# Finding the places of routed results: scatters into four small tables in place of one-hot products

## The chip, the cores and the metric

The kernel runs on one core of a Trainium2 chip. The metric is the device time of one execution in microseconds (us). The profile is of one such execution, and its span is the time from the first to the last instruction that it records.

## What is computed

The input x has 16 sequences of 512 tokens with 256 features. The layer normalises x and adds to x an attention (16 heads of 16, each token sees itself and the 128 before it) and a mixture of experts:

```python
xn = _layernorm(x, axis=-1)
x = x + attn(xn, Wq, bq, Wk, bk, Wv, bv, Wo, bo) + ffn(xn, ...)
# ffn:
logits = xt @ gate_w.T
_, idx = jax.lax.top_k(logits + beta, K)            # K = 2 of E = 8 experts
probs = jax.nn.sigmoid(jnp.take_along_axis(logits, idx, axis=-1))
c = jnp.zeros((B, E), xt.dtype).at[jnp.arange(B)[:, None], idx].add(probs)
h = jax.nn.silu(g) * u                              # g, u: 256 -> 512 of each expert
eo = jnp.einsum('bem,emh->beh', h, down_proj_w)     # 512 -> 256
combined = jnp.einsum('beh,be->bh', eo, c)
return (combined + shared_out).reshape(B0, S0, H0)  # shared_out: one FFN for all tokens
```

There are 8192 tokens, so 16384 results (token, chosen expert) have to be computed, each to be weighted with its probability.

## The kernel before, in words

**Stages.** `norm` (lines 204 to 271) normalises the sequences in groups of three, writes the rows to `xn_d` in HBM, and makes values and routing logits. `route` (325 to 465) chooses the experts. `attention` (625 to 679) works through 64 groups (16 sequences, four head groups each) in five steps per group. `early` (833) computes the shared FFN of one sequence. `experts` (856 to 957) runs over NB = 135 blocks: the results are sorted by expert, every expert's run is rounded up to whole blocks of 128 slots, and a block gathers its 128 rows of `xn_d` by `source` (line 877), turns them on PE, multiplies with the expert's weights (897, 915), and scatters 128 rows of results into `y_d` by `target` (922). `y_d` has two rows for every token. `endings` (961 to 1000) reads for each sequence the sums so far (`acc`) and in two halves its rows of `y_d`, multiplies these rows by `prob` (968), adds both rows of each token (972), and stores.

**How places are found in `route`.** Lines 336 to 408 give for every token and choice a slot number (block times 128 plus lane); token number t x 128 + p and choice k stand in partition p, column (t, k) of `slots`. What the blocks need is the inverse: for each lane and block, which result it is. Lines 429 to 457 get it with 128 products: for each (t, k) VectorE (DVE) builds `hot_l` (128 x 128, 1 where the lane is the result's, line 444) and `hot_b` (128 x 135, the result's number where the block is the result's, line 448), and PE adds `hot_l` transposed times `hot_b` into one bank, `found` (434). Lines 459 to 465 make `target` and `source` of it; a slot that got no result has zero there and is sent to a row that nobody reads.

**The order of the work.** Everything is issued from one loop over `attention` (1054 to 1064), four turns a step, 1304 turns in all, and every engine takes its instructions in the built order. In each turn beside attention's own work: `background` (normalisation, then routing) is advanced one step in five of every eight turns, until it ends; `filling` is advanced `pace` = 0.918 steps; `endings` one step. `filling` (1008 to 1027) runs shared FFNs of whole sequences, 24 steps each, until routing has ended, then all the experts (810 steps), then the remaining shared FFNs; a shared FFN of the sequence that attention works on is held back until attention's part is stored. `endings` starts when the experts are through, eight turns a sequence. When the loop is over, the rest of `filling` and then of `endings` is issued (1067 to 1070). A scheduler that builds the program may move an instruction on its engine within what dependences allow.

**Queues that matter.** GpSimd (POOL) issues the indirect DMAs (877, 922), and between them copies each group's values into place (`spread_values`, 502), adds `bo` to a first `acc` (816), and does the endings' arithmetic. The value copies are needed by PE's products with the values (605), a whole group of 20 turns later. SyncE (SP) issues all other DMAs in order, a wait included. `y_in` has two buffers, `acc` four. A large part of route's scratch lies in the same buffers as the weights (`part_tile`).

Of the kernel before, what the change touches and what calls it, by code (L numbers as in the profile page):

```python
# [41 lines left out]
def block_kernel(ctx: ExitStack, tc: tile.TileContext, a: dict, out: bass.AP):  # L42
# [130 lines left out]
    lane = count("lane", [[1, P]], P)  # L173
    block_no = count("block_no", [[1, NB]], NB)

    result_no = count("result_no", [[1, 2], [2 * P, TT]], 2 * TT, by=2, base=1)
    result_no = result_no.rearrange("p (k t) -> p k t", k=2)
# [133 lines left out]
    prob = const.tile([P, 2, TT], FP, tag="prob", name="prob")  # L311
    expert = const.tile([P, NB], I32, tag="expert", name="expert")
    source = const.tile([P, NB], I32, tag="source", name="source")
    target = const.tile([P, NB], I32, tag="target", name="target")
    no_token = one.tile([P // 2, D], FP, tag="no_token", name="no_token")
    nc.gpsimd.memset(no_token, 0.0)
    nc.sync.dma_start(out=xn_d[TT * P :], in_=no_token)
# [7 lines left out]
    def route():  # L325
# [32 lines left out]
        nc.vector.reciprocal(prob, prob)  # L358

# [43 lines left out]
        for k in range(2):  # L403
# [5 lines left out]
        part = one.tile([P, 2, TT, 2], I32, tag="r_part", name="r_part")  # L409
        nc.vector.tensor_single_scalar(part[:, 0], slots, 7, op=ALU.logical_shift_right)  # L410
        nc.vector.tensor_single_scalar(part[:, 1], slots, P - 1, op=ALU.bitwise_and)
        where = small[:, 2:].rearrange("p a k t -> p a (k t)").rearrange(
            "p a (t k) -> p a t k", k=2
        )
        nc.vector.tensor_copy(where, part)

# [10 lines left out]
        yield  # L427

        found = bank_b()
        ready = []  # L430

        def add_ready():
            for t, k, hot_l, hot_b in ready:
                nc.tensor.matmul(
                    found[:, :NB], lhsT=hot_l, rhs=hot_b,
                    start=t == 0 and k == 0, stop=t == TT - 1 and k == 1,
                )
            ready.clear()

        for t in range(TT):  # L440
            pairs_of = []
            for k in range(2):
                hot_l = six.tile([P, P], FP, tag="hot_l", name="hot_l")
                nc.vector.tensor_scalar(  # L444
                    hot_l, lane, where[:, 1, t, k : k + 1], None, ALU.is_equal
                )
                hot_b = six.tile([P, NB], FP, tag="hot_b", name="hot_b")
                nc.vector.tensor_scalar(  # L448
                    hot_b, block_no, where[:, 0, t, k : k + 1], result_no[:, k, t : t + 1],
                    ALU.is_equal, ALU.mult,  # L450
                )
                pairs_of.append((t, k, hot_l, hot_b))
            add_ready()
            ready.extend(pairs_of)
            if t % 2:
                yield
        add_ready()
        unused = first
        nc.vector.tensor_scalar(
            unused, found[:, :NB], 0.0, unused_no, ALU.is_equal, ALU.mult  # L460
        )
        nc.vector.tensor_tensor(unused, unused, found[:, :NB], ALU.add)
        nc.vector.tensor_scalar_add(unused, unused, -1.0)
        nc.vector.tensor_copy(target, unused)
# [391 lines left out]
    def experts():  # L856
# [53 lines left out]
        def half_down(i, half):  # L910
# [8 lines left out]
            if half == 1:  # L919
                y = three.tile([P, D], FP, tag="y", name="y")  # L920
                nc.scalar.copy(y, sums.pop(i)[:, :D])  # L921
# [39 lines left out]
    def endings():  # L961
        added = []

        def add():
            b, half, acc, y = added.pop()
            tiles = slice(NT // 2 * half, NT // 2 * (half + 1))
            weight = prob[:, :, b * NT : (b + 1) * NT][:, :, tiles].rearrange("p k t -> p t k")
            nc.gpsimd.tensor_tensor(
                y, y, weight.unsqueeze(3).to_broadcast([P, NT // 2, 2, D]), ALU.mult
            )  # L970
# [164 lines left out]
```

## Time and profile before

| | us |
|---|---|
| median of three runs | 1988.27 (1985.82 to 1989.53) |
| the profiled execution | 1989.47 |
| its span | 1987.8 |
| one-hot stage, first `hot_l` to last `hot_b` | 436.7 to 538.6 |
| first expert matmul (897) | 548.5 |
| last scatter into `y_d` starts | 1778.6 |
| endings' arithmetic on POOL (968, 972) | 1784.7 to 1981.1 |
| attention's last reciprocal (622) | 1958.0 |

In a profile line, L448 is line 448 of the kernel; PE is the matrix engine and PEld its weight loads, ACT is ScalarE, SPq and POOLq are DMAs issued by these engines. A group's line gives the engine, the operation, the output and inputs with shapes, xcount, then busy time in us, mean duration in ns, and after the second bar the idle time ahead of it with what ended it. A float32 matmul shows as two records. Busy times of matmuls overlap a little, since they are pipelined. The chain that ended last lies to 88% of the span on PE.

### The profile page before, as it was taken

Reading aid. Unit: us, or ns where it says so; the run is one execution under the profiler, and the core shown is the slowest. Engines: PE = TensorE matmul, PEld = TensorE weight load, DVE = VectorE, ACT = ScalarE, POOL = GpSimd, SP = SyncE. Lnnn points to the kernel's source line nnn. Section 1 sums busy time; section 2 is a strip of 40 time slices with the busy share of each in tenths; the row PEclk is TensorE's granted clock in tenths of the full one; section 3 lists DMA queues with packets and bytes.
Section 4 is the critical chain, followed back from the end, with each engine's and each line's share of the span. In section 5 each row is a group of like instructions: output and inputs, shape, how many; then the busy total and the mean of one; then the engine's idle time right before and its main releaser. Section 6 shows DMA issues by size and latency. Waiting matters only on the chain.

```text
span 1987.8 us, 35311 instructions
## 1 busy us (share of the span) xinstructions
PE 1916.6 (96%) x12011; PEld 1654.5 (83%) x12011; DVE 1211.1 (61%) x3912; ACT 684.6 (34%) x1752; POOL 605.8 (30%) x765
## 2 busy tenths in 40 slices
PE   7899999999899999999999999999999999998985
PEld 4677767767789999999989899998989899985763
DVE  5767756599945565555555566555655565555652
ACT  3333323321133333333333333333333333332320
POOL 5212212210022222222222323222222222228884
PEclk9899999999999999999999999999999999999997
DMA  7634434341257676777676777777676777757774
GB/s 198 196 120 154 151 88 133 128 124 35 59 183 245 204 233 229 223 243 220 208 235 219 223 234 232 218 251 212 217 226 216 225 235 233 217 182 215 228 238 147
DMA packets 355773, 386.58 MB, mean 194 GB/s; under 512 B 118528, under 2 KB 262976, under 8 KB 355584
## 3 DMA queue, kind: packets, MB, share of 16 engines
q1 hardware_dynamic: 342624, 348.82, 55.9%
q0 software_dynamic: 12960, 35.41, 5.5%
q8 instruction: 98, 1.61, 0.3%
q14 instruction: 91, 0.75, 0.1%
HBM read 307.67 MB, written 68.09 MB: 189 GB/s over the span
## 4 chain that ended last, share of the span: by engine, by line
PE 88%; DVE 8%; POOL 1%; DMA 1%; issue 1%; ACT 0%; SPq 0%; POOLq 0%; DVEq 0%; ACTq 0%
PE a L897 24%; PE a L557 13%; PE b L915 12%; PE c L605 12%; PE a L764 9%; PE b L789 5%; PE b L777 3%; PE b L255 3%; PE a L524 2%; PE a L514 2%; PE b L887 2%; DVE hot_b L448 1%; DVE den L622 1%; DVE hot_l L444 1%; DVE probs L546 1%
## 5 line engine op out<-in xcount | busy, mean ns | idle before, releaser
L897 PE MATMUL a<-xgT,w 128*128 128x128 f32 x4320 | 548.7, 276 | 1.9 <-DVE maxima L546 1.0
L897 PEld LDWEIGHTS a<-xgT,w 128*128 128x128 f32 x4320 | 526.9, 193 | 12.7 <-issue 8.5
L550 ACT ACTIVATE probs<-probs,maxima 128x160 f32<-128x160 f32 (+4 forms) x1024 | 346.2, 401 | 528.8 <-DVE maxima L546 508.4
L546 DVE CUSTOM_DVE_ANT_0 probs<-a,window 128x160 f32<-128x160 f32 (+4 forms) x1024 | 254.1, 297 | 235.4 <-PE a L557 225.0
L605 PEld LDWEIGHTS c<-turned,spread_v 128*128 128x128 f32 x2048 | 308.9, 191 | 58.2 <-issue 42.6
L605 PE MATMUL c<-turned,spread_v 128*128 128x160 f32 (+4 forms) x2048 | 338.1, 290 | 10.5 <-DVE ctxT L623 10.1
L557 PE MATMUL a<-kT,spread 128*128 128x160 f32 (+4 forms) x2048 | 323.2, 295 | 0.0
L557 PEld LDWEIGHTS a<-kT,spread 128*128 128x128 f32 x2048 | 290.4, 192 | 33.2 <-issue 25.0
L877 POOL DMA_INDIRECT xg<-xn_d,source x135 | 132.9, 984 | 472.3 <-PE b L887 416.6
L915 PE MATMUL b<-w,hr 128*128 128x256 f32 x1080 | 271.7, 381 | 0.0
L622 DVE RECIPROCAL den<-den 64x512 f32<-64x512 f32 x64 | 214.1, 3346 | 85.3 <-ACT den L617 82.7
L764 PE MATMUL a<-xT,shared 128*128 128x512 f32 x480 | 242.0, 609 | 11.5 <-DMA xT<-xT_d 11.5
L596 DVE STREAM_TRANSPOSE turned<-probs 128x480 f32<-128x480 f32 (+1 forms) x256 | 161.8, 632 | 104.9 <-ACT probs L550 101.5
L502 POOL COPY spread_v<-v 32x256 f32<-32x256 f32 x256 | 101.4, 397 | 373.8 <-PE c L605 219.9
L922 POOL DMA_INDIRECT y_d<-y,target x135 | 132.4, 981 | 266.3 <-ACT y L921 236.5
L915 PEld LDWEIGHTS b<-w,hr 128*128 128x128 f32 x1080 | 189.8, 190 | 19.6 <-issue 2.6
L753 DVE SCALAR_TENSOR_TENSOR hr<-hr,a 128x512 f32<-128x512 f32 x135 | 91.8, 680 | 136.4 <-ACT hr L752 127.8
L789 PE MATMUL b<-shared,h 128*128 128x256 f32 x512 | 133.1, 392 | 4.4 <-DVE acc L794 2.8
L752 ACT ACTIVATE hr<-a 128x512 f32<-128x512 f32 x135 | 79.9, 592 | 149.5 <-PE a L897 142.2
L764 PEld LDWEIGHTS a<-xT,shared 128*128 128x128 f32 x480 | 83.8, 195 | 50.7 <-issue 36.1
L754 DVE SCALAR_TENSOR_TENSOR hr<-hr,a 128x512 f32<-128x512 f32 x135 | 91.8, 680 | 45.9 <-PE a L897 43.0
L789 PEld LDWEIGHTS b<-shared,h 128*128 128x128 f32 x512 | 94.4, 196 | 20.0 <-DVE acc L794 3.5
(141 smaller groups left out, 1701.1 us busy)
## 6 DMA issues: line engine op xcount, KB each, us to landing
w<-in_gp SPq DMA_DIRECT2D x135, 512.0 KB
w<-in_up SPq DMA_DIRECT2D x135, 512.0 KB
w<-in_dp SPq DMA_DIRECT2D x135, 512.0 KB
acc_d<-acc SPq DMA_DIRECT2D x32, 512.0 KB
acc<-acc_d SPq DMA_DIRECT2D x32, 512.0 KB
y_in<-y_d SPq DMA_DIRECT2D x32, 512.0 KB
xT<-xT_d SPq DMA_DIRECT2D x30, 512.0 KB
xn_d<-xn SPq DMA_DIRECT2D x16, 512.0 KB
```

Of the source, the lines that this page charges most:

```text
L546: nc.vector.tensor_tensor_reduce(out=to, in0=ps, in1=window[:, WIN - n :], scale=-SCALE, scalar=-MASKED, op0=ALU.add, op1=ALU.min, accum_o ...
L550: nc.scalar.activation(to, to, AF.Exp, bias=least, scale=-1.0)
L557: nc.tensor.matmul(ps, lhsT=spreads[group % 2][:, u].rearrange("p g q -> p (g q)"), rhs=w["kT"][:, group // 2, f:e], start=True, stop=True,)
L596: nc.vector.transpose(moved(pT, Q * blocks[0] + P * first, [[WIN, n], [P, SEEN], [1, Q]]), moved(pr, 0, [[WIN, n], [Q, SEEN], [1, Q]]),)
L605: nc.tensor.matmul(av[:, Q * k : Q * k + n], lhsT=spread_v[s][:, k], rhs=pT[:, WIN * k : WIN * k + n], start=k == ORDER[0], stop=k == ORDE ...
L622: nc.vector.reciprocal(den[mine], den[mine])
L764: nc.tensor.matmul(ps, lhsT=wt[:, c, ts(m, P)], rhs=xT[:, c], start=c == 0, stop=c == KC - 1,)
L789: nc.tensor.matmul(po[t][:, :D], lhsT=h[m][:, ts(t, P)], rhs=wd[:, m], start=m == 0, stop=m == MC - 1,)
L877: nc.gpsimd.indirect_dma_start(out=g, out_offset=None, in_=xn_d, in_offset=bass.IndirectOffsetOnAxis(ap=source[:, i : i + 1], axis=0),)
L897: nc.tensor.matmul(hidden[i][which][:, ts(m, P)], lhsT=weights[i, which][:, c, ts(m, P)], rhs=turned[i][:, c], start=c == 0, stop=c == KC - 1,
L915: nc.tensor.matmul(po[:, :D], lhsT=made[i][:, ts(m, P)], rhs=weights[i, 2][:, m], start=m == 0, stop=m == MC - 1,)
L922: nc.gpsimd.indirect_dma_start(out=y_d, out_offset=bass.IndirectOffsetOnAxis(ap=target[:, i : i + 1], axis=0), in_=y, in_offset=None,)
```

## The change

Routing no longer builds one-hot matrices. Each result's pair (number, weight) is written by an indirect DMA into its slot's row of a table in HBM. There are 128 such scatters of 128 rows with 8 bytes, issued by POOL two per background step; they go round four tables, so that a table is written by every fourth. The tables are filled with zeros at the start of the kernel. After the scatters SP reads the four tables back into two tiles, DVE adds them (every slot is written in one table, the others hold zero), PE transposes the sum in four pieces, and DVE makes `target`, `source` and a new `share_of` (the weight of each slot) from that. Route has 84 background steps for the 45 before. Since the weight is now known for each slot, ACT scales a block's rows as it takes them from the bank, and the multiply at the endings is dropped. The diff, cut to its core:

```diff
+    pairs = const.tile([P, TT, 2, 2], FP, tag="pairs", name="pairs")
+    nc.gpsimd.tensor_copy(pairs[:, :, :, 0], result_no.rearrange("p (t k) -> p t k", k=2))
...
+    NE = NB + NB % 2
+    share_of = const.tile([P, NE], FP, tag="share_of", name="share_of")
+    nothing = one.tile([NE // 2, 4 * P], FP, tag="nothing", name="nothing")
+    nc.gpsimd.memset(nothing, 0.0)
+    tables = [dram.tile([NE * P, 2], FP, tag=f"table{i}", name="table") for i in range(4)]
+    by_row = lambda t: t.rearrange("(j x) n -> j (x n)", j=NE // 2)
+    for t in tables:
+        nc.sync.dma_start(out=by_row(t), in_=nothing)
...
         nc.vector.reciprocal(prob, prob)
+        nc.vector.tensor_copy(pairs[:, :, :, 1], prob.rearrange("p k t -> p t k"))
...
-        part = one.tile([P, 2, TT, 2], I32, tag="r_part", name="r_part")
-        nc.vector.tensor_single_scalar(part[:, 0], slots, 7, op=ALU.logical_shift_right)
-        nc.vector.tensor_single_scalar(part[:, 1], slots, P - 1, op=ALU.bitwise_and)
-        nc.vector.tensor_copy(where, part)
...
-        for t in range(TT):
-            pairs_of = []
-            for k in range(2):
-                hot_l = six.tile([P, P], FP, tag="hot_l", name="hot_l")
-                nc.vector.tensor_scalar(
-                    hot_l, lane, where[:, 1, t, k : k + 1], None, ALU.is_equal
-                )
-                hot_b = six.tile([P, NB], FP, tag="hot_b", name="hot_b")
-                nc.vector.tensor_scalar(
-                    hot_b, block_no, where[:, 0, t, k : k + 1], result_no[:, k, t : t + 1],
-                    ALU.is_equal, ALU.mult,
-                )
-                pairs_of.append((t, k, hot_l, hot_b))
-            add_ready()
-            ready.extend(pairs_of)
-            if t % 2:
-                yield
+        for t in range(TT):
+            for k in range(2):
+                nc.gpsimd.indirect_dma_start(
+                    out=tables[(2 * t + k) % len(tables)],
+                    out_offset=bass.IndirectOffsetOnAxis(ap=slots[:, t, k : k + 1], axis=0),
+                    in_=pairs[:, t, k], in_offset=None,
+                )
+            yield
+        yield
+        rows = [part_tile(i, "rows")[: NE // 2] for i in range(2)]
+        for i, t in enumerate(tables):
+            nc.sync.dma_start(out=rows[i // 2][:, ts(i % 2, 4 * P)], in_=by_row(t))
+        for _ in range(4):
+            yield
+        low, high = (r[:, : 4 * P] for r in rows)
+        for r in rows:
+            nc.vector.tensor_tensor(r[:, : 4 * P], r[:, : 4 * P], r[:, 4 * P :], ALU.add)
+        entry = rows[0][:, 4 * P :]
+        nc.vector.tensor_tensor(
+            entry.rearrange("j (n h x) -> j h x n", n=2, h=2),
+            low.rearrange("j (h x n) -> j h x n", n=2, h=2),
+            high.rearrange("j (h x n) -> j h x n", n=2, h=2), ALU.add,
+        )
+        yield
+        found = bank_b()[:, : 2 * NE]
+        for i in range(4):
+            nc.tensor.transpose(
+                found[:, ts(i, NE // 2)], entry[:, ts(i, P)], ident[: NE // 2, : NE // 2]
+            )
+        yield
...
-                nc.scalar.copy(y, sums.pop(i)[:, :D])
+                nc.scalar.mul(y, sums.pop(i)[:, :D], share_of[:, i : i + 1])
...
-            weight = prob[:, :, b * NT : (b + 1) * NT][:, :, tiles].rearrange("p k t -> p t k")
-            nc.gpsimd.tensor_tensor(
-                y, y, weight.unsqueeze(3).to_broadcast([P, NT // 2, 2, D]), ALU.mult
-            )
             for k in range(2):
                 nc.gpsimd.tensor_tensor(acc[:, tiles], acc[:, tiles], y[:, :, k], ALU.add)
```

## The prediction

> **What bounds the kernel now.** I read the page first: its busy totals and the span in 40 slices (49.7 us each).
>
> ```profile
> PE 1916.6 (96%) x12011; PEld 1654.5 (83%) x12011; DVE 1211.1 (61%) x3912; ACT 684.6 (34%) x1752; POOL 605.8 (30%) x765
> ...
> DVE  5767756599945565555555566555655565555652
> POOL 5212212210022222222222323222222222228884
> ```
>
> PE is the bound nearly everywhere. Two places differ: slices 8 to 10, where DVE is full and POOL idle, and the last four, where POOL is at 8. The busy time by stretches, columns PE, PEld, DVE, ACT, POOL, then granted clock, DMA share and GB/s:
>
> ```profile
> 333.00:436.00 103.00, 102.92 (x481) 75.66 (x480) 78.39 (x222) 32.62 (x87) 22.01 (x33) 1.00 0.34 102
> 436.00:540.00 104.00, 95.66 (x541) 77.86 (x541) 101.64 (x400) 20.37 (x52) 3.88 (x10) 0.95 0.21 64
> 563.65:676.05 112.40, 112.00 (x810) 104.86 (x809) 61.29 (x202) 42.34 (x108) 28.62 (x37) 1.00 0.70 229
> ```
>
> The middle row is the stage that the change replaces: DVE 101.6 of 104 us. The groups by line say with what, and show the other lines the change touches:
>
> ```profile
> L502 POOL COPY spread_v<-v 32x256 f32<-32x256 f32 x256 | 101.4, 397 | 373.8 <-PE c L605 219.9 <-DMA y_d<-y,target 75.7 <-issue 39.1
> L972 POOL TENSOR_TENSOR acc<-acc,y_in 128x512 f32<-128x512 f32 x64 | 80.9, 1267 | 18.3 <-issue 11.5 <-DMA acc<-acc_d 2.8
> L968 POOL TENSOR_TENSOR y_in<-y_in,prob 128x1024 f32<-128x1024 f32 x32 | 60.8, 1901 | 27.7 <-DMA y_in<-y_d 27.4
> L448 DVE TENSOR_SCALAR hot_b<-block_no,r_f,result_no 128x135 f32<-128x135 f32 x128 | 43.8, 342 | 0.0
> L434 PE MATMUL b<-hot_b,hot_l 128*128 128x135 f32 x256 | 42.0, 286 | 0.8 <-DVE hot_b L448 0.8
> L444 DVE TENSOR_SCALAR hot_l<-lane,r_f 128x128 f32<-128x128 f32 x128 | 35.0, 273 | 0.0
> ```
>
> The timeline of POOL in two short windows prices an indirect DMA (columns: start, duration, line; in brackets the idle time before):
>
> ```profile
> 545.16 0.94 POOL L877 DMA_INDIRECT xg<-xn_d,source  x1 [0.31 <-issue]
> 546.41 0.95 POOL L877 DMA_INDIRECT xg<-xn_d,source  x1 [0.30 <-issue]
> ...
> 837.33 0.97 POOL L922 DMA_INDIRECT y_d<-y,target  x1 [1.15 <-ACT y L921]
> 838.35 0.39 POOL L502 COPY spread_v<-v 32x256 f32<-32x256 f32 x1
> 842.29 1.26 POOL L502 COPY spread_v<-v 32x256 f32<-32x256 f32 x3 [3.55 <-DMA y_d<-y,target]
> ```
>
> Two back to back are 1.25 us apart, and after a scatter the second value copy (L502) starts only when it has landed: 842.29 - 837.33 = 5.0 us. Last, the tail after the final matmul (1967.9):
>
> ```profile
> 1968.38 0.37 SPq L827 DMA_DIRECT2D acc_d<-acc  x1
> 1972.11 0.37 SPq L813 DMA_DIRECT2D acc<-acc_d  x1
> 1976.17 4.92 POOL L972 TENSOR_TENSOR acc<-acc,y_in 128x512 f32<-128x512 f32 x4 [8.15 <-issue]
> 1981.11 0.38 SPq L827 DMA_DIRECT2D out<-acc  x1
> ```
>
> One sequence's sums go out and back, then one store: 20 us. The execution took 1989.5 us, 1.7 over its span, and lies at the top of the three runs (median 1988.3). The sum below is made against this execution.
>
> **Part 1: the one-hot products go.** Removed: 78.8 us of DVE (43.8 + 35.0) and 42.0 us of PE records. In the stretch 436 to 540 PE executed 541 records, 256 of them these. The other 285 at the 0.214 us of the row above (102.92 / 481) are 61 us: 43 us gained. Adding up PE's columns in built order (eight records of 512 columns take 3.43 us, so 1.67 ns per column of a two-record matmul, times 1.04 for what PE loses in a loaded stage) gives the same picture: 161 us of columns lie between the first hot matmul (437.3) and the changed kernel's first expert matmul, so unhindered that falls at 437 + 168 = 605. It comes later than now (548.5) only because three more shared FFNs are put before it (part 3).
>
> **Part 2: 128 scatters on POOL's queue.** Each is one DMA_INDIRECT. A scatter into a table waits for the one before into the same table, so at most four are under way: the pitch is the larger of 1.27 us (0.97 + 0.30) and a quarter of the landing, 5.0/4 = 1.25. I take 1.3. The trace has no 8-byte scatter; the bounds are 0.97 (no gap) and 9.0/4 = 2.25 (the longest landing in the trace, 1040.10 to 1049.09), and I stay by the commonest row. 128 x 1.3 = 166 us on an engine that PE's schedule gives about 140 (102 turns of the main loop at 1.4).
>
> What is queued behind them is the point: POOL runs in order, and the value copies L502 that every head group's PE products (L605) need stand between the scatters. In the built order the copies for groups 12, 13, 14, 15 and 16 come after 4, 38, 82, 120 and 128 scatters, and each waits until the scatters before it have landed (3.7 us beyond its own first copy, with the copies 5 us). Scatters start when the slots are ready (cast L408, 434.2). Copies ready: group 12 at 445; group 13, 34 x 1.3 + one bias add L816 (2.4) + 5 later, 497; group 14, 44 x 1.3 + 4.7 + 5, 564; group 15, 38 x 1.3 + 5, 618.5; the last eight land at 633. PE, unhindered, wants group 13 at 493, 14 32 us later, 15 another 24 later, 16 another 25 later. So it waits 3.5 us, then 564 - 529 = 35, then 618.5 - 588 = 30.5, and 16 (due 643) not at all: 70 us lost, since PE too is in order. What is late next: the reading back. SP's four loads wait for the last scatters, and behind them stand an acc store and the query spreads; DVE's adds wait for the loads, and behind them stands the softmax. Landing at 633 comes before PE reaches that place (about 645), so they cost nothing; without that cover, 8 us. First expert matmul: 605 + 70 = 675.
>
> Two rules of the Trainium skill are weighed here. "SBUF — State Buffer", section on its two separate sides, warns that an indirect DMA's descriptors cannot be written while DVE holds the shared port: 620 ns alone, 3100 ns beside a DVE copy. That would make 128 x 3.1 = 397 us, over 230 more. The row speaks otherwise: L922's 135 scatters took 965 to 1005 ns beside a DVE busy 55%, so I leave it out. "DMA: Bandwidth & Descriptors", anatomy of one DMA, gives a fixed 2.0 us to land; by it each copy waits 3 us less and the sum falls by some 14. The trace's 5.0 decides.
>
> **Part 3: the later start of the experts.** Routing gets 5 of 8 turns; normalisation's 135 steps end at turn 216. Route had 45 steps (to turn 288) and has 84 (64 scatter steps for 32, plus 7; to 351). Until then the filling runs shared FFNs, 24 steps each at 0.918 per turn, and finishes the one begun: experts start at turn 366 instead of 288 and, with 810 steps, end at 1248 instead of 1170. Attention has 1304 turns. Endings take 8 turns a sequence: 134 were left for 16 of them; now 56, which is seven. Nine sequences' endings, and the shared FFN of the last, stand behind attention with no matmul beside them. The expert stage itself keeps its length, 1772 - 548.5 = 1223.5 (columns within 0.2%): it ends at 675 + 1225 = 1900. Then PE has 68 us of columns (169 before, which took 196 us with waits for xT, y_in and the last softmax); with 1.03 and 12 us of such waits, 82: last matmul at 1982.
>
> The tail: SP's order has the last shared FFN's store, which waits for PE, ahead of the remaining loads, so the first of nine stores goes at once and eight follow at a pace. Per sequence: store issue 0.4, load issue 0.5, landing 4.5 (1832.3 to 1836.8 in the trace), then two adds of 1.27, with 0.1: 8.1 us; two y buffers allow no more overlap. 9.7 + 7 x 8.1 + 6.7 (the last store to the end, 1981.1 to 1987.8) = 73 us, where now 20 follow the last matmul. The dropped multiply L968 (60.8 us of POOL, 1.9 per half) is already out of this; without that the pace would be 10.
>
> **At nothing:** ACT's multiply by a column for the copy L921 (L848 with a column takes 722 ns for 512 elements, a plain copy 585: about +70 ns of 256, 9 us in all, under PE; ACT is 38% busy); bounds 0 and 9. The fills of the tables and pairs at the start, 4 issues and about 1 us of POOL before PE's first work depends on little else: 0 to 3. The final adds, four transposes and casts, under 6 us of DVE in a stage that has lost 79.
>
> **The sum.** 675 + 1225 + 82 + 73 = 2055 of span, 2056 us. As differences: about -45, +70, +53 in the tail, less some 10 in the shorter last stretch.
>
> **Rivals.** (a) The scatters are hidden: place, POOL's queue between groups 12 and 16. If eight bytes per row are cheaper than a kilobyte, below 0.72 us each (434.5 + 28 + 120p = 549 when group 15 is due), no group waits: 2056 - 70 = 1986, no change; and with landings 0.6 us shorter in the emptied tail, 1982, faster. Against it: 0.98 us in the mean of 270 instances, and the number of rows stays 128. (b) Landing sets the pitch, 2.0 us, since small rows land late: 128 x 0.7 = 90 more, 2146. For it: landings of 9.0; against: the DMA share is 0.21 to 0.34 there. (c) The groups' slack takes half of the stall, or the tail paces at POOL's 5.1 us (2 x 2 x 1.27): 2020. Against the last: a transfer never landed under 3.7 us, with one buffer ahead.
>
> **Chances.** Likeliest 0.62 (2025 to 2095 for pitch 1.1 to 1.5); (b) 0.12; (c) 0.14; (a) 0.12, of it 0.07 faster and 0.05 the same. A measurement of this kernel can tell about 0.2% (4 us) from no change. So slower 0.88. The range 2005 to 2115 takes in (c) and leaves out (a) and most of (b).
>
> **What would show it.** Right: 128 new DMA_INDIRECT at 1.2 to 1.4 us pitch in 435 to 630, PE's L605 idle there for POOL's value copies, 60 to 75 us; a first expert matmul near 675; after the last matmul some 70 us of adds on POOL waiting for y_in. Wrong: PE idle under 20 us in that stage, a pitch near 0.7 or above 1.8, or a tail under 40 us, which would mean that endings ran under attention after all.

## The result, and the profile after

The changed kernel takes 2103.9 us (median of 4 runs, 2102.4 to 2104.1), the kernel before 1988.5: a ratio of 1.0584, 95% interval 1.0569 to 1.0599, so 5.8% slower. The profiled execution has a span of 2102.2 us. The forecast was 2056 us with a range of 2005 to 2115: the direction and the three mechanisms held, and the time is 48 us above the predicted one, so the loss is 115 us where some 67 were forecast.

The page's busy totals and three rows of its 40 slices (52.6 us each), of the changed kernel:

```profile
PE 1885.6 (90%) x11759; PEld 1624.0 (77%) x11759; DVE 1154.7 (55%) x3658; ACT 696.1 (33%) x1752; POOL 668.7 (32%) x861
...
PE   7899999997427999999999999999999999999920
...
POOL 5212221345772122222222222222322322221555
PEclk9999999998768999999999999999999999999965
```

PE has 31 us less to do (1916.6 before) and DVE 56 us less, and yet the span grew by 114. Two holes in PE's row say where: slices 10 to 12, counted from one, where POOL is at 5 to 7 and the granted clock goes down with PE's row, and the last two, where POOL works at 5 and PE at 2 and then not at all.

The first hole, in the groups by line: the two groups of matmuls that PE idles ahead of, then the scatters' own line.

```profile
L608 PE MATMUL c<-turned,spread_v 128*128 128x160 f32 (+4 forms) x2048 | 339.0, 291 | 46.6 <-POOL spread_v L505 42.4
...
L767 PE MATMUL a<-xT,shared 128*128 128x512 f32 x480 | 241.3, 608 | 57.2 <-DMA xT<-xT_d 54.0
...
L432 POOL DMA_INDIRECT table<-pairs,slots x128 | 122.9, 960 | 56.9 <-issue 37.5
```

In the timeline of PE from 437 to 720 us (start, duration, line; in brackets the idle time before) three lines hold most of it:

```profile
511.69 0.90 PE L608 MATMUL c<-turned,spread_v 128*128 128x160 f32 x2 [15.57 <-POOL spread_v L505]
...
576.84 1.44 PE L608 MATMUL c<-turned,spread_v 128*128 128x160 f32 x4 [26.86 <-POOL spread_v L505]
...
640.81 2.04 PE L767 MATMUL a<-xT,shared 128*128 128x512 f32 x2 [48.22 <-DMA xT<-xT_d]
```

Two stalls wait for value copies on POOL, the third, the longest, for a load. POOL's timeline between (the scatters left out here: 38 stand between the copies at 575.52 and 625.27) and SP's own show why:

```profile
573.60 0.40 POOL L505 COPY spread_v<-v 32x256 f32<-32x256 f32 x1
575.52 1.26 POOL L505 COPY spread_v<-v 32x256 f32<-32x256 f32 x3 [1.52 <-issue]
...
625.27 0.39 POOL L505 COPY spread_v<-v 32x256 f32<-32x256 f32 x1
628.81 1.26 POOL L505 COPY spread_v<-v 32x256 f32<-32x256 f32 x3 [3.15 <-DMA table<-pairs,slots]
```

```profile
523.25 0.36 SPq L816 DMA_DIRECT2D acc<-acc_d  x1
630.10 0.85 SPq L537 DMA_DIRECT2D v<-v_d  x2
631.07 2.55 SPq L497 DMA_DIRECT2D spread<-qT  x4
633.99 0.85 SPq L537 DMA_DIRECT2D v<-v_d  x2
634.94 1.43 SPq L803 DMA_DIRECT2D xT<-xT_d  x2
```

SP issues nothing for 106 us. The next thing in its order is the load of a sequence's values `v` (L537). It goes at 630.10, when POOL's last copy out of `v` has ended (628.81 + 1.26 = 630.07); the query spreads and the load of xT (L803) stand behind it in the same queue. xT lands when PE goes on, at 640.8. That the load waits for the copies is what a later run's profile names; that it does so because `v` has one buffer is not shown (see the run with two buffers).

The second hole is the tail. From the chain that ended last (start, duration, what):

```profile
2028.90 0.45 SPq L830
2029.35 0.05 issue
2029.40 7.04 DMA y_in<-y_d
2036.45 0.07 issue
2036.52 1.27 POOL acc L971
2037.79 0.07 issue
2037.85 1.27 POOL acc L971
2039.14 0.38 SPq L830
```

One store, one load, two adds, and the next store, 10.2 us later. Seven more stores follow at 7.65 us each, and from the last (2092.7) to the end of the span it is 9.5 us. The forecast against the trace:

| step | forecast | measured |
|---|---|---|
| pitch of a scatter | 1.3 us | 1.26 (0.96 + 0.30) in an unbroken row |
| first and last scatter | 434.5 to about 630 | 438.6 to 639.8 |
| PE's stalls | 3.5 + 35 + 30.5 = 69, taken as 70 | 15.6 + 26.9 + 48.2 = 90.7 |
| first expert matmul | 675 | 716.3 |
| length of the experts | 1225 | 1221.6 |
| last expert matmul to last matmul | 82 | 90 |
| last matmul to the end | 73 | 74 |

### The profile page after: what moved, and what is told of

Read it like the earlier page. It is cut to its first block, busy times and chain, and to the rows that moved or that the text cites. A ratio compares the mean times of both kernels' runs of the same rounds, so it can differ in the third digit from the quotient of the medians.

```text
span 2102.2 us, 34660 instructions
## 1 busy us (share of the span) xinstructions
PE 1885.6 (90%) x11759; PEld 1624.0 (77%) x11759; DVE 1154.7 (55%) x3658; ACT 696.1 (33%) x1752; POOL 668.7 (32%) x861
## 4 chain that ended last, share of the span: by engine, by line
PE 62%; DMA 4%; POOL 4%; issue 1%; DVE 1%; SPq 0%; ACT 0%; POOLq 0%; DVEq 0%; ACTq 0%
PE a L900 23%; PE b L918 11%; PE a L560 9%; PE c L608 9%; DMA y_in<-y_d 3%; PE b L780 2%; POOL table L432 2%; POOL acc L971 2%; PE a L527 2%; PE a L517 2%; PE b L890 1%; PE a L767 1%; PE b L792 1%; DMA table<-pairs,slots 0%; DMA rows<-table 0%
## 5 line engine op out<-in xcount | busy, mean ns | idle before, releaser
L900 PEld LDWEIGHTS a<-xgT,w 128*128 128x128 f32 x4320 | 524.4, 192 | 10.7 <-issue 5.7
L608 PEld LDWEIGHTS c<-turned,spread_v 128*128 128x128 f32 x2048 | 311.4, 192 | 99.9 <-issue 46.2
L608 PE MATMUL c<-turned,spread_v 128*128 128x160 f32 (+4 forms) x2048 | 339.0, 291 | 46.6 <-POOL spread_v L505 42.4
L560 PE MATMUL a<-kT,spread 128*128 128x160 f32 (+4 forms) x2048 | 323.1, 296 | 2.1 <-DMA spread<-qT 2.1
L560 PEld LDWEIGHTS a<-kT,spread 128*128 128x128 f32 x2048 | 291.3, 193 | 36.2 <-issue 25.7
L767 PE MATMUL a<-xT,shared 128*128 128x512 f32 x480 | 241.3, 608 | 57.2 <-DMA xT<-xT_d 54.0
L767 PEld LDWEIGHTS a<-xT,shared 128*128 128x128 f32 x480 | 84.0, 194 | 96.5 <-issue 83.6
L432 POOL DMA_INDIRECT table<-pairs,slots x128 | 122.9, 960 | 56.9 <-issue 37.5
L792 PE MATMUL b<-shared,h 128*128 128x256 f32 x512 | 133.0, 396 | 6.8 <-DVE acc L797 4.2
```

Of the source, the lines that this page charges most:

```text
L432: nc.gpsimd.indirect_dma_start(out=tables[(2 * t + k) % len(tables)], out_offset=bass.IndirectOffsetOnAxis(ap=slots[:, t, k : k + 1], axis=0),
L560: nc.tensor.matmul(ps, lhsT=spreads[group % 2][:, u].rearrange("p g q -> p (g q)"), rhs=w["kT"][:, group // 2, f:e], start=True, stop=True,)
L608: nc.tensor.matmul(av[:, Q * k : Q * k + n], lhsT=spread_v[s][:, k], rhs=pT[:, WIN * k : WIN * k + n], start=k == ORDER[0], stop=k == ORDE ...
L767: nc.tensor.matmul(ps, lhsT=wt[:, c, ts(m, P)], rhs=xT[:, c], start=c == 0, stop=c == KC - 1,)
L792: nc.tensor.matmul(po[t][:, :D], lhsT=h[m][:, ts(t, P)], rhs=wd[:, m], start=m == 0, stop=m == MC - 1,)
L900: nc.tensor.matmul(hidden[i][which][:, ts(m, P)], lhsT=weights[i, which][:, c, ts(m, P)], rhs=turned[i][:, c], start=c == 0, stop=c == KC - 1,
```

## The experiments

In each, "before" is the kernel before on the same chip. The runs are told in the order of what they settle.

### Without the scatters

```diff
         for t in range(TT):
             for k in range(2):
+                if t:
+                    continue
                 nc.gpsimd.indirect_dma_start(
...
-                    in_=y_d[r0 : r0 + P * NT].rearrange("(t p k) d -> p t (k d)", p=P, k=2),
+                    in_=xn_d[r0 // 4 : r0 // 4 + P * NT].rearrange("(t p k) d -> p t (k d)", p=P, k=2),
```

> The changed kernel with 126 of its 128 scatters left out (nearly all slots then count as unused, and the endings read normalised rows in place of results, so its output is not the layer's). All other work, the read back, the 84 steps and the order stay. Theory A (PE waits for POOL's queue of scatters, and the later experts leave nine endings after attention): PE's stalls of some 90 us in 437 to 641 and their aftermath go, first expert matmul near 605, tail still 73: 1990, from 1980 to 2005. Rival B (the read back and the adds, a chain of loads, delay the experts whatever the number of scatters): 2060 or more. Rival C (all of the loss is POOL's, the tail costs nothing against before): 1945.

Measured: 1997.3 us (1993.5 to 1998.9), ratio 1.0054 (1.0037 to 1.0071). As theory A had it. 126 instructions on POOL account for some 106 of the 115 us that the change costs. What is left without them is a kernel with 44.6 us less of matmul time (1872.0 for 1916.6) that is not faster: the experts start 58 us later than before all the same (606.0 for 548.5, with three shared FFNs ahead of them), and after the last matmul come 73 us of endings. The stretch from 437 us to the first expert matmul, of this run and then of the changed kernel (length, then busy us and instructions of PE, PEld, DVE, ACT and POOL, granted clock, DMA share, GB/s):

```profile
437.00:606.00 169.00, 167.95 (x779) 122.18 (x778) 115.54 (x364) 53.54 (x136) 22.68 (x35) 1.00 0.33 91
```

```profile
437.00:716.30 279.30, 179.74 (x782) 128.90 (x782) 116.55 (x366) 54.00 (x137) 144.47 (x162) 0.82 0.24 57
```

PE has the same work in both, 779 and 782 instructions. Without scatters it is done at 606.0; the forecast said 605 for an unhindered PE. With them it takes 110.3 us longer: 98.5 us more idle, and 11.8 us because the same matmuls take longer at a clock of 0.82. The first matmuls after a stall show it: two of L767 take 2.04 us at 640.81 (shown above), and half of that in a running stage. A wait of 3.12 us was already enough:

```profile
542.13 2.07 PE L767 MATMUL a<-xT,shared 128*128 128x512 f32 x2 [3.12 <-DVE maxima L549]
...
548.95 1.02 PE L767 MATMUL a<-xT,shared 128*128 128x512 f32 x2
```

### A later start alone

The kernel before, with 39 empty background steps behind the products:

```diff
         nc.vector.tensor_single_scalar(source, target, 1, op=ALU.logical_shift_right)
+        for _ in range(39):
+            yield
```

> The kernel before with 39 empty background steps after its place finding, so that its route has the 84 steps of the changed kernel; nothing else is changed. Theory A: experts start 78 turns later with three shared FFNs put ahead of them, and nine sequences' endings stand behind attention; POOL still multiplies, so a sequence takes 10 us there and not 7.7: last matmul some 20 us earlier than now, then 85 to 95 us of tail where 20 follow now: 2040, from 2025 to 2060. Rival C (endings run under attention anyway): within 5 us of 1988.

Measured: 2059.9 us (2058.4 to 2060.7), ratio 1.0366 (1.0349 to 1.0383), 72.6 us over before, at the upper edge of A. No work is added: the experts start at 647.1 in place of 548.5 and end at 1868.4 in place of 1771.7, and the endings find no room. In the chain of this run a sequence has one more link, the multiply (L970 here), and the pace is 9.6 us in the mean:

```profile
2002.09 0.38 SPq L829
2002.51 4.59 DMA y_in<-y_d
2007.10 0.07 issue
2007.17 1.91 POOL y_in L970
2009.15 1.26 POOL acc L974
2010.50 1.26 POOL acc L974
2011.78 0.38 SPq L829
```

The changed kernel has 7.65 us for the same, so the dropped multiply is worth 2 us in each sequence that ends alone.

With the run before, this splits the change in three: the later start costs 72.6 us; beside the later start, products and multiply gone are worth 62.6 (1997.3 for 2059.9); the scatters cost 106.6 (2103.9 for 1997.3). Taking the one-hot products out did pay; the longer routing alone costs more than that.

### The value copies on ACT

```diff
-            nc.gpsimd.tensor_copy(
+            nc.scalar.copy(
                 spread_v[s][ts(g, Q), :, at : at + DK], w["v"][ts(g, Q), :, group]
```

The same edit was made to the kernel before, as a control: 1991.9 us (1985.3 to 1995.7), ratio 1.0021 (1.0012 to 1.0030), within the 10 us expected.

> Control of the run with copies on ACT: the kernel before with its value copies on ACT in place of POOL. 256 copies of about 0.3 us (75 us in all) on an engine that is 34% busy, and POOL loses 101 us. All theories: within 10 us of 1988; a few us less if the two waits of PE for POOL near the end (5.7 us) go.

In the changed kernel:

> The changed kernel with the value copies (spread_values) on ACT in place of POOL; the 128 scatters stay on POOL, free of copies between them. Theory A: PE no longer waits for copies or, through the value loads, for xT; POOL ends its scatters near 607 (434.5 + 128 x 1.27 + 10 for bias adds and landings), PE would want the read back near 585, so 20 to 35 us of stall stay of 90: 2035, from 2015 to 2055. Rival B (the length of the scattering itself holds the experts, the copies do not matter): above 2085.

Measured: 2096.4 us (2084.3 to 2115.5), ratio 1.0575 (1.0504 to 1.0647), not clear of the changed kernel's 2103.9. Theory A fell: no matmul waits for POOL's copies now, and the experts start 22 us earlier (694.6), but 89 of the 110 us of delay remain (694.6 - 606.0) in another form. PE's timeline between 584 and 593 us:

```profile
586.32 0.43 PE L608 MATMUL c<-turned,spread_v 128*128 128x160 f32 x1 [1.50 <-issue]
588.42 0.42 PE L608 MATMUL c<-turned,spread_v 128*128 128x160 f32 x1 [1.67 <-issue]
590.52 0.43 PE L608 MATMUL c<-turned,spread_v 128*128 128x160 f32 x1 [1.68 <-issue]
```

These matmuls, four of which take 0.71 us in a running stage, come one in 2.1 us, in steps that are multiples of 0.70 us, with nothing that the profile shows to wait for. Between 437 and 640 us PE's weight loads have 29.4 us of such gaps ahead of L608, 20.1 ahead of L792, 17.1 and 15.0 ahead of L767 and L560; DVE and ACT have them too. The same weight loads have 0.2 us each, at most 0.5, in the changed kernel, where PE rested in its stalls. Rival B, which expected over 2085, named the number and not this. What it is was taken up again below.

### A second buffer for v

```diff
-        w["v"] = one.tile([P, NU, 4, DK], FP, tag="v", name="v")
+        w["v"] = two.tile([P, NU, 4, DK], FP, tag="v", name="v")
```

> The changed kernel with two buffers for the tile of values v in place of one. Theory A (in the changed kernel the third stall, 48.2 us before 640.81, is not the late value copy itself but SP's queue: the load of v waits there until POOL has made the copies of group 15 at 628.8, and behind it stand the query spreads and the load of xT that PE waits for, landed 640.8): with a second buffer the load of v is not held, xT is there early, and the third stall ends when the copies are there, near 629, 12 us sooner: 2091 us (2083 to 2097). Rival B (POOL's queue alone sets the length; SP is idle anyway and only reports it): no difference, 2101 to 2107.

Measured: 2099.4 us (2097.2 to 2103.3), ratio 1.0576 (1.0558 to 1.0594), against 2103.9 for the changed kernel. It does not decide: the load of `v` was not freed by the second buffer. SP's waits between 500 and 660 us (total, times, longest):

```profile
SPq L537 <- POOL spread_v L505: 105.4, 1, 105.4
```

It waited as long as ever for a copy on POOL, and PE's third stall, 49.7 us, ended with xT. So the wait is real, but one buffer is not its whole reason; the rest of the reason stays open. The scatters began 4.8 us earlier in this run (433.8), which is about all of the difference.

### A faster pace of the experts

```diff
-        owed += pace
+        owed += 1.01 if routed and not all_routed else pace
```

> The changed kernel with the filling advanced 1.01 steps a turn while the experts run (0.918 before), so that they end at turn 1168 and all endings find room beside attention. Theory A (the later start costs what it costs through the endings that stand alone behind the last matmul): the stalls of the scatter stage stay (85 to 95 us of PE idle), the 74 us behind the last matmul become 20 to 25, 2053 us (2040 to 2065). Rival B (endings beside attention only move their waits to y_in and acc in front of PE's work): the tail goes but the last stretch before it grows by as much, above 2085.

Measured: 2076.4 us (2069.9 to 2078.1), ratio 1.0447 (1.0423 to 1.0471): 27.5 us gained where A had 50. The last matmul now ends 7 us before the end, but ahead of it PE waits 49 us in the last stretch, 29.5 of them for DVE's sums of the attention (L783) and 14.9 for its products with the reciprocal (L626), where the changed kernel has 14.5 and nothing. So half of A, half of B. Why half follows from the next table. From the last expert matmul to the end of the span, with PE's busy time inside:

| kernel | from, us | length | PE busy |
|---|---|---|---|
| before | 1771.7 | 216.1 | 181.1 |
| changed | 1937.9 | 164.3 | 73 |
| without scatters | 1827.0 | 164.7 | 73 |
| faster pace 1.01 | 1894.0 | 180.0 | 123.9 |
| pinned and spaced, 1.1 (below) | 1856.2 | 177.1 | 95.7 |
| v loaded by POOL, 1.2 (below) | 1807.6 | 216.9 | 142.9 |

With all the endings behind the experts, sixteen sequences at 8 to 10 us each, that stretch was never under 164 us in this table and never under 161 in any run (the one with two buffers for `v`), however little PE had left. The kernel before has 181 us of matmuls beside it. The change does three of those shared FFNs ahead of the experts, so the stretch stays and its cover is gone.

### Spacing the scatters, undone by the scheduler

```diff
             yield
+            if t % 2:
+                yield
...
-        owed += pace
+        owed += 1.1 if routed and not all_routed else pace
```

> The changed kernel with 128 scatters in 96 background steps in place of 64 (0.83 scatters a turn in place of 1.25; about one in 1.7 us, where one takes 1.26), and 1.1 filling steps a turn while the experts run. Theory A (PE is held only where more scatters are asked of POOL than it can issue between two value copies): PE idle in the scatter stage under 15 us, the tail near 25 us, and the gain of 76 us of matmuls and weight loads of the one-hot products is seen at last: 1975 us (1955 to 2000). Rival B (what the run with the value copies on ACT showed is general: beside 128 scatters the instructions of PE, DVE and ACT come late whatever stands in POOL's queue, some 80 us in all): 2030 us or more. Rival C (only the tail goes, as in the run with the faster pace alone): 2045 to 2060.

Measured: 2112.6 us (2110.3 to 2115.4), ratio 1.0641 (1.0623 to 1.0659). B's number (2030 or more) is met, but not for B's reason, since no matmul of this run came late without a wait, and A and C missed: the edit did not space the scatters. Between POOL's value copies stand again 34, 44, 38 and 8 scatters, as in the changed kernel, and PE idles 98.8 us from 437 to the first expert matmul. The scheduler fills POOL's queue with whatever is ready, whatever step of the loop it was built in. Beside the pace, the only effect seen of more steps was that more shared FFNs ran first: the experts start at 784.4 (716.9 in the run before), end 36 us later, and so does the kernel.

### Scatters of 64 rows

```diff
-                    out_offset=bass.IndirectOffsetOnAxis(ap=slots[:, t, k : k + 1], axis=0),
-                    in_=pairs[:, t, k], in_offset=None,
+                    out_offset=bass.IndirectOffsetOnAxis(ap=slots[: P // 2, t, k : k + 1], axis=0),
+                    in_=pairs[: P // 2, t, k], in_offset=None,
...
-                    in_=y_d[r0 : r0 + P * NT].rearrange("(t p k) d -> p t (k d)", p=P, k=2),
+                    in_=xn_d[r0 // 4 : r0 // 4 + P * NT].rearrange("(t p k) d -> p t (k d)", p=P, k=2),
```

> The changed kernel with each of the 128 scatters cut to the first 64 of its 128 rows; half of the slots stay without a result, and the endings read normalised rows in place of the experts' results, so half of the routing's outcome is left out. Theory A (an indirect DMA costs POOL its 0.96 us and the 0.30 after it as an instruction, whatever its rows): pitch 1.2 to 1.3, stalls 75 to 95 us, 2090 to 2106. Rival B (the price is per row: the descriptors are written one by one): duration near 0.5, pitch 0.65 to 0.8, stalls under 25 us, 2030 us (2015 to 2050).

Measured: 2078.1 us (2074.5 to 2080.3), ratio 1.0466 (1.0449 to 1.0483). Theory A holds for the instruction: with half of the rows its median is 892 ns against 958, and the gap stays 0.30, so the price is nearly all per instruction. It misses the total by 12 us (2090 was its lower end): waits for landings fell from 17.1 to 2.1 us at the scatters and from 8.4 to 4.0 at the copies, so 128 scatters took 171 us in place of 201, and the experts started 31 us earlier. Of those 30 us (201 - 171), 8 are the shorter instructions, 15 the scatters' landing waits, 4 the copies'.

### Pinning the scatters behind the copies

Each scatter is kept behind what was built before it on POOL. With a pace of 1.01:

```diff
-                nc.gpsimd.indirect_dma_start(
+                tc.keep_in_program_order(nc.gpsimd.indirect_dma_start(
...
-        owed += pace
+        owed += 1.01 if routed and not all_routed else pace
```

> The changed kernel with the faster pace (1.01) of the experts and one thing more: every scatter is pinned on POOL's queue behind what the loop has traced there before it, so that the scheduler cannot move scatters ahead of value copies. Built order of scatters between the value copies of successive head groups: 28, 24, 24, 26, 22 (in the changed kernel and in the runs so far 34, 44, 38, 8). Theory A (the scheduler's order of POOL is what makes the hold so long: 38 and 44 scatters ahead of a copy): a group's 24 to 26 scatters and its copies take 1.3 x 25 + 5 = 37 us where PE's own work takes 26 to 30, so PE loses 8 to 10 us in each of five groups, 45 in place of 100: 2076 - 55 = 2021 us (2008 to 2040). Rival B (the sum of POOL's work decides and its order only moves the loss): 2065 to 2085. Rival C (the issue of PE is slowed beside scatters, as with the copies on ACT): above 2045, with PE gaps that have no releaser.

Measured: 2059.5 us (2054.5 to 2063.9), ratio 1.0369 (1.0349 to 1.0388). 17 us gained over the same pace without pins (2076.4), where A had 55; PE's idle time from 437 to the first expert matmul is 84.3 us for 101.1. PE's timeline has where it went:

```profile
497.56 0.90 PE L608 MATMUL c<-turned,spread_v 128*128 128x160 f32 x2 [4.61 <-POOL spread_v L505]
535.31 1.44 PE L608 MATMUL c<-turned,spread_v 128*128 128x160 f32 x4 [4.43 <-POOL spread_v L505]
581.25 2.04 PE L767 MATMUL a<-xT,shared 128*128 128x512 f32 x2 [33.01 <-DMA xT<-xT_d]
651.06 2.08 PE L792 MATMUL b<-shared,h 128*128 128x256 f32 x4 [40.65 <-DVE acc L797]
```

The waits for copies are down to 9 us. The 33 us are SP's queue again (the load of `v` goes at 568.70, xT at 573.55). The 40.7 us are new: DVE waits there 37.8 us for the tables' rows (L447), which SP can load only when the scatters into a table have landed, from 637.30 on, and the sum that PE needs stands behind that on DVE. With PE less late, the reading back is late next. A and B missed; C's number (above 2045) is met without its sign, since PE has no gap without a releaser here. The order alone does not settle it.

With 96 steps and a pace of 1.1, so that the pinned order has 16 to 18 scatters to a group and the reading back comes later in the order:

> As the run before it, with the scatters in 96 steps and the experts' pace 1.1, as in the spaced run, whose spacing the scheduler had undone (its order on POOL was that of the changed kernel). Built order now: 18, 16, 16, 18, 16, 16, 16, 8 scatters between the copies of successive groups. Theory A (PE is held only where POOL has more to issue between two copies than fits into a group): 17 x 1.3 + 5 = 27 us against 26 to 30 of PE, so PE idle in the scatter stage falls from 100 to under 25 us: 2112.6 - 85 = 2028 us (2005 to 2045). Rival C (issue slowed beside scatters): over 2060, with PE gaps of 0.7 us and more that have no releaser while POOL scatters.

Measured: 2035.8 us (2026.8 to 2045.5), ratio 1.0244 (1.0200 to 1.0289), 76.8 us less than with the same steps and pace unpinned. The total is theory A's. The stretch from 437 to the first expert matmul:

```profile
437.00:709.40 272.40, 240.51 (x1072) 171.67 (x1070) 154.94 (x490) 74.26 (x187) 151.31 (x171) 0.94 0.31 74
```

All 128 scatters are still there, POOL is busy 151 us, and PE idles 31.9 us where it idled 98.8 (A had under 25). From 560 to 640 us PE is busy 80.0 of 80 us while POOL runs 59 instructions, indirect DMAs, copies and additions of `bo`. So it is not the scatters that hold PE, and not POOL's load; it is how many stand ahead of a copy. What is left is one stall of 14.0 us and one of 17.9, both for xT. SP's timeline has the cause of the first:

```profile
538.04 0.86 SPq L539 DMA_DIRECT2D v<-v_d  x2
539.02 2.56 SPq L499 DMA_DIRECT2D spread<-qT  x4
541.94 0.85 SPq L539 DMA_DIRECT2D v<-v_d  x2
542.90 1.84 SPq L805 DMA_DIRECT2D xT<-xT_d  x2
```

The value copies end at 538.01, the load of `v` goes at 538.04, xT five us later, and PE goes on at 549.49. At the second, xT stands behind the loads of the tables as well: these go at 663.93, xT at 670.62.

### The load of v on POOL's own queue, and the copies on ACT once more

Both keep the pins and the 96 steps and take a pace of 1.2. In the first, POOL issues the load of `v`:

```diff
-            nc.sync.dma_start(
+            nc.gpsimd.dma_start(
                 out=w["v"][ts(g, Q)],
```

> The pinned and spaced scatters with two edits: the four loads of a sequence's values v are issued by POOL in place of SP, and the pace is 1.2 in place of 1.1. Value copies stay on POOL. Theory A (what is left of the hold in the pinned and spaced run, 14 us at 549 and 18 us at 677, is SP's queue: the load of v waits there for POOL's copies and the load of xT stands behind it): on POOL's own queue that load has nothing to wait for that is not done, both stalls go, and the faster pace brings the endings forward: 2035.8 - 30 - 10 = 1996 us (1980 to 2012). Rival B (POOL's copies come late themselves, and SP only shows it): stalls of 20 us or more ahead of the products with the values, 2015 to 2035.

Measured: 2032.2 us (2026.2 to 2036.1), ratio 1.0239 (1.0217 to 1.0260).

```profile
437.00:697.30 260.30, 239.26 (x1046) 170.56 (x1044) 145.76 (x467) 70.61 (x179) 153.65 (x175) 0.97 0.32 75
```

For the stage theory A holds: no stall for xT is left, and the idle time is 21.0 us. The experts end at 1807.6, 49 us earlier than in the run before. But the end did not move beyond the spread of the runs (2035.8 there, 2026.8 to 2045.5). The pace is likely too high; the load of `v` on POOL with the pace of 1.1 was not run. With the experts gone attention runs alone, 217 us of which PE works 143, and its last links wait for one another (20.2 us for DVE's products of context and reciprocal, 22.0 for its sums). The forecast of 1996 took the gain in the stage for a gain at the end.

In the second, ACT copies the values, and a one-element copy on POOL that reads ACT's result keeps the pinned scatters at the pace of the groups:

```diff
-            nc.gpsimd.tensor_copy(
+            nc.scalar.copy(
                 spread_v[s][ts(g, Q), :, at : at + DK], w["v"][ts(g, Q), :, group]
             )
+        nc.gpsimd.tensor_copy(seen, spread_v[s][:1, 0, HALF * s : HALF * s + 1])
```

> The pinned and spaced scatters of the last run, with three edits: value copies on ACT, a one-element copy on POOL that reads what ACT has copied for the group (so that the pinned scatters keep the pace of the groups: 18, 16, 16, 18, 16, 16, 16, 8), and a pace of 1.2. It asks why the run with all value copies on ACT lost as much as the changed kernel although no copy stood in POOL's queue: there POOL had scatters in one unbroken row, and PE, DVE, ACT and SP issued late with nothing to wait for. Theory A (it is the unbroken row of scatters that starves the other engines' issue; sixteen at a time do not): no such gaps, PE idle under 15 us between 437 and the first expert matmul, and no wait of SP for POOL ahead of xT: 2000 us (1980 to 2015). Rival B (it is ACT's copies beside the scatters, spaced or not): gaps of 0.7 us and more without a releaser, 30 us or more of them, above 2025.

Measured: 2047.5 us (2041.9 to 2051.4), ratio 1.0299 (1.0277 to 1.0322). Neither theory holds, though the number is B's. The gaps without a releaser are there, so it is not the unbroken row alone that makes them; but PE's matmuls have only some 13 us of them between 437 and 720 (3.4 at 535, 5.5 from 545 to 551, 0.7 at 604, 3.8 from 638 to 647), not 30. The run with `v` on POOL's queue has 6 us of them, the one before it none over 0.25 us. What causes them stays open: that they come with the scatters is shown (none in the run without them, none with ACT's copies in the kernel before), but not with the scatters alone: the changed kernel and the six runs that leave the copies on POOL and the load of `v` on SP have none ahead of a matmul. Most came with an unbroken row and the copies on ACT; through what they reach the issue of other engines no run here tells.

## Why the prediction was right, and where its sum was short

**DVE's and PE's relief: right.** The unhindered first expert matmul was put at 605, and the run without scatters has it at 606.0. The experts' length is off by 3 us, the multiply by a column on ACT costs 100 ns (473 for 373), under PE, as said.

**The pitch: right.** 1.26 for 1.3, and the instruction's longest time was 1.16 us beside a DVE that was busy 33% from 437 to 640 us, and 1.15 in the pinned and spaced run beside 58% (437 to 665). So the row was the better guide here than 3.1 us for each, which would have made 397. Rival (b), landing sets the pitch at 2.0, is refuted: four tables' landings cost 17 us in all, not 90. Rival (a), a scatter below 0.72 us because its rows are short, is refuted by the 0.96 itself; even half of the rows take 0.89.

**"So it waits 3.5 us, then 564 - 529 = 35, then 618.5 - 588 = 30.5": the step that was short.** The mechanism, copies behind scatters on POOL, is what the traces show, with the 4, 34, 44, 38 and 8 scatters that the forecast had counted, and pinning and spacing the scatters takes most of it away. But the three waits are 15.6, 26.9 and 48.2. Three terms are missing or too small:
- The start. Scatters began at 438.6, not 434.2, and the forecast gave those ahead of group 13 an even pitch, where 15 of the 17 us of landing waits fall among them; group 13 was ready at about 511.6 for 497. That is the first 12 us. The 5 us for the landing and the copies was too much in turn: from the end of the last scatter's 1.26 us to the last of a group's copies the trace has 4.9, 2.3, 2.9 and 4.5 for groups 12 to 15.
- **SP's queue.** The forecast named the loads of the tables as what SP has late, and found them covered. It did not follow the other load that waits for POOL: that of `v`, ahead of the query spreads and xT. The third stall thus stops PE at a product with xT, 15.8 us after the second stall and not 24, and ends at 640.8, 10.7 us after the copies of group 15, not with them; the SP lines of the pinned and spaced run show the same chain alone, and with the load on POOL's queue the wait for xT is gone.
- The clock. For some us after a stall matmuls run at half speed (2.04 us for 1.02), and the granted clock is 0.67 from 560 to 600 us. The same 780 instructions took 11.8 us more. The Trainium skill says this ("TensorE: Matmul & The Clock Gate", Part 1: after an idle window of about 3.4 us the array runs at half clock until it has been busy for as long); here 3.12 us of waiting were enough. The forecast counted idle time and not what follows it: three stalls of over 15 us each take a few us more than their length.

The second stall is 8 us shorter than forecast by luck: PE came to it 38.3 us after the first (511.7 to 550.0) and not 32, held up by a wait of 3.1 us and by the slow clock, and the copies of group 14 took 65 us after those of group 13, for 67.

The stalls make 90.7, small waits 7.8 and the clock 11.8: 110 where 70 was put, 40 of the 48 us. The other 8 are the last stretch, 90 for 82, with one wait of 14.5 us for a sum (L783) that POOL's addition of `bo` to `acc` releases (L819, 2007.8 to 2010.2). That addition stands behind the endings' adds on POOL, and its load behind an ending's store on SP.

**The reading back "comes before PE reaches that place ... so they cost nothing": right here, by its cover.** In the changed kernel nothing of PE's waits is put down to it. In the run with pinned scatters, where PE came sooner, the cover was gone and it cost 40.7 us, not the 8 that the forecast had put for that case.

**The tail: right in cause, and in size by two errors that cancel.** 74 for 73: 7.65 for 8.1 us a sequence saves 3 us, and from the last store to the end it is 9.5 us for 6.7. And the kernel before, with nothing but a later start, loses 72.6 us. The half of rival (c) in which the tail paces at POOL's 5.1 us is refuted; its other half, that slack takes half of the stall, is refuted by the stall's 90.7.

## What to carry to other kernels

An instruction that costs 1.26 us of an idle engine is not free if the same engine's queue holds a small copy that the bound engine needs: count how many of the new ones the scheduler puts ahead of each copy (34, 44 and 38 here), and pin and space them before counting the gain: spacing alone left the order as it was, pinning alone gave 17 us at the same pace, pinning the spaced scatters 77. Follow each wait one queue further: a load that waits for that copy holds what stands behind it on SP. Work that is taken from beside a chain of loads and adds does not shorten that chain: look at how long it takes with little beside it (164 us here), and keep as much of the bound engine's work for it. None of the variants came below the kernel before. The nearest of the changed kernel with all of the work is that with the load of `v` on POOL's queue, 2.4% above.

## What the runs showed of the hardware

- An indirect DMA of 128 rows with 8 bytes occupies POOL for 0.96 us and 0.30 until the next, one of 64 rows 0.89 and 0.30; the kilobyte rows of L922 in the kernel before took 0.98. Neither the bytes nor the number of rows sets more than a few hundredths of a us of it.
- With the value copies on ACT and an unbroken row of scatters on POOL, PE issued in many places between 500 and 640 us in steps that are multiples of 0.70 us (ACT and SP in one such step with it, at 591.23), with no wait that the profile shows. With the start of the experts at 694.6 for 606.0 it cost most of what the edit had freed, and its cause was not found.
- After waits of 3.12 us and longer PE's first matmuls took twice their time (2.07 us for 1.02), after one of 0.96 us they did not (eight of L792 at 587.46 took 2.04 us; four take 1.03).
